# Layer 1 of a two-layer convolution kernel: a ring buffer for the spline features, a new layout for the SiLU scratch, shared row loads and another order of the DMA queue

## The chip, the core and the metric

The kernel runs on one core of one Trainium2 chip. The metric is the time of one execution on the device in microseconds (us); shorter is better. An execution is one program: it reads its inputs from HBM, computes both layers for all four images and writes the output back to HBM. A few tensors in HBM are scratch that one part of the program writes and a later part reads.

## The reference

The input x has 4 images of 16 channels of 256 by 256 in float32. There are two layers, each of which adds to x what it computes from a group-normalised x:

```python
# layer 0
x = x + _L0_conv_ref(_gn(x), conv_w, conv_b)   # 3x3 conv to 400 logits, softmax over 25 taps, weighted 5x5 sum
# layer 1
x = x + _L1_conv_ref(_gn(x), base_weight, spline_weight, spline_scaler, bias_weight)
...
    patches = _extract_patches(x, KSIZE, STRIDE, PAD)            # 3x3, zero padding
    bspl = _b_splines(patches, grid)                             # 8 cubic B-spline bases
    out = jnp.einsum('bjhwn,ijn->bihw', jax.nn.silu(patches), base_w)
    out = out + jnp.einsum('bjhwns,ijns->bihw', bspl, spl_w)
    out = out + bias_weight[None, :, None, None]
```

Layer 1, which the change is about, is thus a 3x3 convolution over 9 maps for each input channel: the SiLU of the normalised pixel and its 8 spline bases.

## The kernel before, in words

Layer 0 works in 64 strips (image, half of the rows, 32 columns). TensorE makes the logits (L773, L777), ScalarE their exponentials (L796), GpSimd multiplies them by the pixels (L801), VectorE sums (L677). The SyncE queue (SP) loads its operands ahead. The result of layer 0, x1, goes to an HBM scratch `x1s` (channel, row, column). In the last strips, `scales(0)` turns the statistics of image 0 into the scale and shift that layer 1 needs, one small step at a time.

Layer 1 works in 64 units: image b, and a block u of 16 rows. For unit n the code of `layer1` does, on several engines:

- `load_x(n)` (L867): one DMA of 2048 KB, x1s into `xt`. Each of the 16 channels is written to 8 partitions (128 in all), one for each spline basis, so each partition gets the same run of 16 rows, 16 KB. Three buffers, `xta`, `xtb`, `xtc`.
- `features(n)` (L902): on ScalarE the absolute value with scale and shift (L908), on both halves of the rows, then `spline` (L155): three activations on ScalarE (L158 to L160) and four operations on VectorE (L161 to L164). The result goes into a feature tile `fa`, `fb` or `fc` of 18 rows by 258 columns, the columns 0 and 257 holding padding.
- `halo(n)` (L911): the first two rows of a feature tile are the last two of the one before; a DMA from SBUF to SBUF copies them (L917), and GpSimd writes padding at the edge of an image.
- SiLU: `load_rows(n, xsp, "xs")` loads the unit's 16 rows in another layout (8 rows by 16 channels on the partitions, two DMAs of 128 KB), `silu` (L883) applies the activation in place on ScalarE three units ahead, `put_silu` (L887) writes it to the HBM scratch `sls` in two DMAs, and `load_silu(n)` (L894) reads it back in four DMAs, one for each of the four input rows of a pair of output rows, into `sl` (64 partitions). The scratch has 1 KB rows; the zero row above and below an image is written once, in layer 0 (L816).
- `outputs(n)` (L931): 96 matmuls on the features (L937) and 24 on `sl` (L945), in float32, into one PSUM tile.
- The residual: `load_rows(n, xrp, "xr")` loads the same 16 rows once more, `put` (L923), two units later, adds the PSUM tile, the bias and the residual on VectorE (L925) and stores the result in two DMAs (L927).

The order of all engines' queues is written by hand: `in_order` keeps the instructions of each engine in the order of the code. For SP a unit of the loop (L978 to L999) is: `load_x(n+2)`, halo of n, `put_silu(n+2)` (two DMAs), `xs` rows of n+5 (two), `xr` rows of n (two), the store of n-2 (two), `load_silu(n+1)` (four): 14 DMAs. In the built program there are eight semaphores for SP's DMAs, used in turn, and each DMA waits for the one before it on its own semaphore, so at most eight DMAs of this queue are under way. VectorE's order is: one step of `scales` for one of the images 1 to 3 (L980), features of n, then the `put` of n-2.

Of the kernel before, what the change touches and what calls it, by code (L numbers as in the profile page):

```python
# [33 lines left out]
def conv_preact_kernel(  # L34
# [14 lines left out]
    G = 8  # L49
# [27 lines left out]
    XA = 5  # L77
    NU = H // RU
    LAG1 = 2
# [12 lines left out]
    sls = [dram.tile([C, CP], F32, name=f"sls{b}") for b in range(B)]  # L92
# [33 lines left out]
    zrow = const.tile([C, W], F32, name="zrow")  # L126
    nc.gpsimd.memset(zrow, 0.0)
# [38 lines left out]
    def scales(b, psum):  # L166


        def small(n, name):
            return stat1.tile([P, n], F32, name=f"{name}_{b}", tag=name)  # L170

        mv = stat1.tile([P, G, 2], F32, name=f"mv_{b}", tag="mv")
        for g in range(G):
            nc.vector.bn_aggr(mv[:, g, :], st1[b][:, g].rearrange("p n s -> p (n s)"))
        yield
        ps = psum()[:, 0:G]
        nc.tensor.matmul(ps, lhsT=ones, rhs=mv[:, :, 0], start=True, stop=True)
        yield
        mean, d, rstd = small(G, "mean"), small(G, "d"), small(G, "rstd")
        q = stat1.tile([P, 6], F32, name=f"q_{b}", tag=f"q{b}")  # L180
        nc.vector.tensor_sub(d, mv[:, :, 0], ps)
        nc.vector.tensor_mul(mean, gsel_sb, ps)
        nc.vector.reduce_sum(q[:, 1:2], mean, AX.X)
        yield
        nc.scalar.activation(d, d, AF.Square)
        yield
        ps = psum()[:, 0:G]
        nc.tensor.matmul(ps, lhsT=ones, rhs=d, start=True, stop=False)
        nc.tensor.matmul(ps, lhsT=ones, rhs=mv[:, :, 1], start=False, stop=True)
        yield  # L190
        nc.vector.tensor_scalar(rstd, ps, EPS, None, ALU.add)  # L191
        yield
        nc.gpsimd.tensor_tensor(rstd, rstd, mhalf, ALU.pow)  # L193
        nc.gpsimd.tensor_mul(rstd, rstd, gsel_sb)
        yield
        nc.vector.reduce_sum(q[:, 0:1], rstd, AX.X)
        nc.vector.tensor_scalar(q[:, 1:2], q[:, 1:2], q[:, 0:1], -1.0, ALU.mult, ALU.mult)
        for k in range(2):
            nc.vector.tensor_scalar(q[:, 2 + k : 3 + k], q[:, k : k + 1], 2.5, None, ALU.mult)
        yield  # L200
        ps = psum()[:, 0:2]
        nc.tensor.matmul(
            ps, lhsT=sel.rearrange("p c s -> p (c s)"), rhs=q[0:C, 2:4], start=True, stop=True
        )
        yield
        nc.vector.tensor_copy(q[:, 4:5], ps[:, 0:1])
        nc.vector.tensor_add(q[:, 5:6], ps[:, 1:2], ub)
        sc[b] = tuple(q[:, k : k + 1] for k in (0, 1, 4, 5))
        yield
# [179 lines left out]
    with tc.tile_pool(name="prep0", bufs=2) as prep, tc.tile_pool(  # L389
# [91 lines left out]
        def prepare1():  # L481

            nc.gpsimd.tensor_mul(sw, sw, ss)
            wc = pre.tile([P, 3, nm], F32, name="wc")
            for d in range(3):
                nc.vector.tensor_reduce(
                    wc[:, d], sw[:, d].rearrange("p k j -> p j k"), AX.X, ALU.add
                )
            nc.vector.tensor_scalar(wc, wc, -1.0 / 6.0, None, ALU.mult)
            wb1 = pre.tile([nm, nm], F32, name="wb1")  # L490
            nc.vector.tensor_reduce(wb1, bw.rearrange("p k j -> p j k"), AX.X, ALU.add)
            for r in range(RT):
                nc.vector.tensor_copy(
                    wt[:, r : r + 3, :, r, :], wc.rearrange("p d (e o) -> p d e o", e=3)
                )
                nc.sync.dma_start(
                    ws[r * C : (r + 3) * C, :, r, :], wb1.rearrange("p (e o) -> p e o", e=3)
                )
# [96 lines left out]
    def layer0(shift):  # L595
# [4 lines left out]
        with tc.tile_pool(name=f"prep{arm}", bufs=2) as prep, tc.tile_pool(  # L600
# [136 lines left out]
            for n, (b, hf, s) in enumerate(strips):  # L737
                if (hf, s) == (0, 0):
# [3 lines left out]
                    if b == B - 1:  # L742
                        first_scales = scales(0, lambda: ptr.tile(
                            [P, QG, P], F32, name=f"ps0{arm}", tag="tp"
                        )[:, 0])
# [9 lines left out]
                for j in range(0, SW, JG):  # L755
# [55 lines left out]
                    if b == B - 1 and j == 0 and s > 0:  # L811
                        next(first_scales, None)
                if n == 0:
                    for t in sls:
                        for r in (0, H + 1):
                            nc.sync.dma_start(t[:, r * W : (r + 1) * W], zrow)  # L816
# [11 lines left out]
    def layer1(arm, last, marks):  # L828
# [3 lines left out]
        with ExitStack() as pools:  # L832
# [13 lines left out]
            XT, FT = [P, RU + 1, W], [P, RU + 2, W + 2]  # L846
            xt0, tmp0, xsp = fixed("xta", XT), temps("ta"), pool("xs", XA)
            f0, xrp = fixed("fa", FT), pool("xr", LAG1 + 2)
            tmp1, xt1, f1 = temps("tb"), fixed("xtb", XT), fixed("fb", FT)
            sl = fixed("sl", [RD * C, RU // RT, W + 2], 2)  # L850
            xtt, fb = xt0 + xt1 + fixed("xtc", XT), f0 + f1 + fixed("fc", FT)
# [12 lines left out]

            def load_x(n):  # L867
                b, u = units[n]
                lo, hi = span(u)
                nc.sync.dma_start(  # L870
                    xtt[n % 3][:, 0 : hi - lo, :],
                    rows(x1s[b], [[CP, C], [0, NS], [1, (hi - lo) * W]], u * RU - 1 + lo),
                )


            def load_rows(n, p, name):
                b, u = units[n]
                t = p.tile([P, 2, W], F32, name=f"{name}_{n}{arm}", tag=name)
# [4 lines left out]
            def silu(n, t):  # L883
                b, u = units[n]
                nc.scalar.activation(t, t, AF.Silu, scale=sc[b][0], bias=sc[b][1])

            def put_silu(n, t):  # L887
                b, u = units[n]
                for g in range(2):
                    nc.sync.dma_start(  # L890
                        rows(sls[b], [[W, 8], [CP, C], [1, W]], 1 + u * RU + 8 * g), t[:, g]
                    )

            def load_silu(n):  # L894
                b, u = units[n]
                for d in range(RD):
                    nc.sync.dma_start(
                        sl[n % 2][d * C : (d + 1) * C, :, 1 : W + 1],
                        rows(sls[b], [[CP, C], [RT * W, RU // RT], [1, W]], u * RU + d),
                    )  # L900

            def features(n):  # L902
                b, u = units[n]
                lo, hi = span(u)
                mid = (lo + hi + 1) // 2
                for (a, z), tmp in (((lo, mid), tmp0), ((mid, hi), tmp1)):
                    xt = xtt[n % 3][:, a - lo : z - lo]
                    nc.scalar.activation(xt, xt, AF.Abs, scale=sc[b][2], bias=sc[b][3])  # L908
                    spline(fb[n % 3][:, a:z, 1 : W + 1], xt, *(t[:, 0 : z - a, :] for t in tmp))

            def halo(n):  # L911
                b, u = units[n]
                f = fb[n % 3]
                if u == 0:
                    nc.gpsimd.tensor_copy(f[:, 0, :], pad)
                else:
                    nc.sync.dma_start(f[:, 0:2, :], fb[(n - 1) % 3][:, RU : RU + 2, :])  # L917
                if u == NU - 1:
                    nc.gpsimd.tensor_copy(f[:, RU + 1, :], pad)  # L919
# [3 lines left out]
            def put():  # L923
                b, u, yp, xr = waiting.pop(0)
                nc.vector.scalar_tensor_tensor(xr, yp, bias_sb, xr, ALU.add, ALU.add)  # L925
                for g in range(2):
                    nc.sync.dma_start(  # L927
                        rows(out[b], [[W, 8], [H * W, C], [1, W]], u * RU + 8 * g), xr[:, g]
                    )

            def outputs(n, xr):  # L931
                b, u = units[n]
                yp = py.tile([P, 2, W], F32, name=f"yp_{n}{arm}", tag="yp")
                M = RT * C
                for k, (d, e) in enumerate((d, e) for d in range(RD) for e in range(3)):
                    for t in range(NT):
# [3 lines left out]
                            rhs=fb[n % 3][:, t * RT + d : t * RT + d + 9 : 8, e : e + W],  # L940
                            start=k == 0, stop=False,
                        )
                for e in range(3):
                    for t in range(NT):
# [3 lines left out]
                            rhs=sl[n % 2][:, t : t + NT + 1 : NT, e : e + W],  # L948
# [6 lines left out]
                for b in range(1, B)  # L955
            ))
            load_x(0)
            ss = [load_rows(n, xsp, "xs") for n in range(XA)]
            load_x(1)
            nc.gpsimd.tensor_copy(pad, edge[:, 4:5].to_broadcast([P, W + 2]))  # L960
            for t in fb:
                for e in (0, W + 1):
                    nc.gpsimd.tensor_copy(
                        t[:, :, e : e + 1],
                        edge[:, 4:5].unsqueeze(2).to_broadcast([P, RU + 2, 1]),
                    )
            for t in sl:
                for e in (0, W + 1):
                    nc.gpsimd.memset(t[:, :, e : e + 1], 0.0)
            features(0)  # L970
            first_silu = len(nc.cur_bb.bb.instructions)
            for n in range(SA):
                t = ss.pop(0)
                silu(n, t)
                put_silu(n, t)
            load_silu(0)
            made = []
            for n in range(len(units)):  # L978
                if n > 0:
                    next(more, None)  # L980
                    features(n)
                if n + 2 < len(units):
                    load_x(n + 2)
# [3 lines left out]
                made = []  # L987
                if n + SA < len(units):
                    t = ss.pop(0)
                    silu(n + SA, t)  # L990
                    made.append((n + SA, t))
                if n + XA < len(units):
                    ss.append(load_rows(n + XA, xsp, "xs"))
                xr = load_rows(n, xrp, "xr")
                if len(waiting) >= LAG1:
                    put()
                if n + 1 < len(units):
                    load_silu(n + 1)
                outputs(n, xr)  # L999
            while waiting:  # L1000
                put()
# [57 lines left out]
```

## Time and profile before

| | |
|---|---|
| median of 3 runs | 3414.09 us (3395.18 to 3421.41) |
| the profiled execution's own time | 3413.86 us |
| its span, first to last instruction | 3412.1 us |
| busy, whole span: TensorE / VectorE / ScalarE / GpSimd | 2853.5 / 3100.7 / 2135.2 / 1935.3 us |
| granted TensorE clock, mean | 0.91 |
| DMA | 687.47 MB in 405554 packets, mean 201 GB/s |
| VectorE's last instruction of layer 0 / first of layer 1's features | 2102.50 us (L697; its statistics follow at 2104.82) / 2107.45 us (L161) |
| first `put` on VectorE / the 61st | 2157.55 us / 3367.25 us |

The span falls into three parts: up to about 130 us the inputs, statistics and weights, then layer 0 up to about 2107 us, then layer 1. "Busy" counts compute instructions; a DMA-issuing instruction on SP isn't counted as busy. The DMA share is the mean over the core's 16 DMA engines. A wait names the instruction or the DMA whose end came last before it ended. The DMA records of the trace hold each packet's start, duration and size.

### The profile page before, as it was taken

The numbers are of one execution on the slowest core, as the hardware profiler recorded it, in microseconds if no ns is written. First come the engines' busy times: TensorE is split into PE (matmuls) and PEld (weight loads), VectorE is DVE, ScalarE is ACT, GpSimd is POOL, SyncE is SP. The second block draws the span as 40 slices with busy tenths as digits, with TensorE's granted clock in tenths as the row PEclk, the third lists the DMA queues.
The fourth block names the chain that finished last, engine by engine and source line by source line (L and its number), as shares of the span: only waits on it lengthen the run. The fifth ranks groups of instructions, "written<-read, shape, count | busy, mean of one in ns | idle before, by whom it ended". The sixth has DMA issues, their size and how long they took to land.

```text
span 3412.1 us, 39823 instructions
## 1 busy us (share of the span) xinstructions
PE 2853.5 (84%) x14264; PEld 1509.4 (44%) x14264; DVE 3100.7 (91%) x1799; ACT 2135.2 (63%) x2233; POOL 1935.3 (57%) x647
## 2 busy tenths in 40 slices
PE   4499999999999999999999995677777777777778
PEld 3366665666655566566566552122222222222222
DVE  6599999999999999999999999877887888878886
ACT  6365654555644565554444446787887777778775
POOL 2299999999999999999999995000000000000000
PEclk7699999999999999999999997888888888888889
DMA  7998887888787798777766667888888888888885
GB/s 229 286 235 221 228 223 200 210 208 245 213 222 192 198 241 239 202 203 192 183 166 180 180 157 159 188 197 195 198 197 193 191 190 194 196 194 192 192 198 131
DMA packets 405554, 687.47 MB, mean 201 GB/s; under 512 B 47986, under 2 KB 274788, under 8 KB 397156
## 3 DMA queue, kind: packets, MB, share of 16 engines
q1 hardware_dynamic: 372324, 668.05, 78.6%
q10 hardware_dynamic: 33024, 16.78, 1.7%
q8 instruction: 117, 1.92, 0.3%
q14 instruction: 89, 0.73, 0.1%
HBM read 547.64 MB, written 121.15 MB: 196 GB/s over the span
## 4 chain that ended last, share of the span: by engine, by line
DVE 53%; DMA 34%; PE 5%; SPq 4%; issue 3%; ACT 1%; POOL 1%; ACTq 0%; DVEq 0%; POOLq 0%
DVE nd L677 45%; DMA xr<-x1s 8%; DMA sl<-sls 7%; DMA xs<-x1s 5%; DMA xtb<-x1s 4%; DMA xtc<-x1s 3%; PE lg L773 2%; DMA sls<-xs 2%; PE yp L937 1%; DMA xin<-in_x_dram 1%; DVE r L696 1%; DMA fc<-fb 1%; DVE st L711 1%; DVE nd L695 1%; SPq L880 1%
## 5 line engine op out<-in xcount | busy, mean ns | idle before, releaser
L773 PE MATMUL lg<-wm,am 128*128 128x400 f32 x4096 | 1748.4, 508 | 123.4 <-ACT e L796 109.2
L801 POOL TENSOR_TENSOR e<-e,u 128x1600 f32<-128x1600 f32 x512 | 1789.0, 3538 | 67.2 <-ACT e L796 66.8
L677 DVE TENSOR_REDUCE nd<-e 128x128 f32<-128x3200 f32 x512 | 1747.0, 3476 | 21.7 <-POOL e L801 21.6
L796 ACT ACTIVATE e<-lg 128x800 f32<-128x800 f32 x1024 | 815.6, 836 | 896.4 <-DVE nd L677 782.9
L777 PE MATMUL lg<-wn,an 97*128 97x400 f32 x2048 | 1358.5, 663 | 0.0
L773 PEld LDWEIGHTS lg<-wm,am 128*128 128x128 f32 x4096 | 766.3, 194 | 450.3 <-ACT e L796 159.6
L777 PEld LDWEIGHTS lg<-wn,an 97*128 97x128 f32 x2048 | 390.9, 191 | 309.8 <-issue 13.4
L937 PE MATMUL yp<-fa,wt 128*32 128x512 f32 x2112 | 278.8, 687 | 134.5 <-DMA fa<-fc 89.2
L937 PE MATMUL yp<-fb,wt 128*32 128x512 f32 x2016 | 259.7, 677 | 110.4 <-DMA fb<-fa 98.8
L937 PE MATMUL yp<-fc,wt 128*32 128x512 f32 x2016 | 260.7, 679 | 102.1 <-DMA fc<-fb 102.1
L919 POOL COPY fa<-pad 128x258 f32<-128x258 f32 x2 | 3.4, 1704 | 477.3 <-DMA xr<-x1s 315.5
L937 PEld LDWEIGHTS yp<-fa,wt 128*32 128x32 f32 x2112 | 82.6, 123 | 327.7 <-issue 279.7
L937 PEld LDWEIGHTS yp<-fb,wt 128*32 128x32 f32 x2016 | 79.4, 122 | 288.2 <-issue 288.2
L937 PEld LDWEIGHTS yp<-fc,wt 128*32 128x32 f32 x2016 | 79.6, 122 | 280.6 <-issue 274.0
L193 POOL TENSOR_TENSOR rstd<-rstd,mhalf 128x8 f32<-128x8 f32 x4 | 9.3, 2332 | 340.4 <-DVE rstd L191 340.4
L919 POOL COPY fc<-pad 128x258 f32<-128x258 f32 x1 | 1.5, 1474 | 319.6 <-DMA fa<-fc 319.6
L945 PE MATMUL yp<-sl,ws 64*32 64x512 f32 x1536 | 178.1, 592 | 0.0
L163 DVE TENSOR_TENSOR ta<-ta,ta 128x2048 f32<-128x2048 f32 (+1 forms) x64 | 147.3, 2302 | 0.0
L163 DVE TENSOR_TENSOR tb<-tb,tb 128x2048 f32<-128x2048 f32 x64 | 145.3, 2271 | 0.0
L908 ACT ACTIVATE xta<-xta,q 128x2048 f32<-128x2048 f32 (+2 forms) x44 | 92.0, 2090 | 82.0 <-DMA xta<-x1s 82.0
L908 ACT ACTIVATE xtb<-xtb,q 128x2048 f32<-128x2048 f32 (+2 forms) x42 | 87.8, 2091 | 83.7 <-DMA xtb<-x1s 83.7
L908 ACT ACTIVATE xtc<-xtc,q 128x2048 f32<-128x2048 f32 (+2 forms) x42 | 87.8, 2091 | 81.3 <-DMA xtc<-x1s 81.3
(184 smaller groups left out, 2605.0 us busy)
## 6 DMA issues: line engine op xcount, KB each, us to landing
am<-hst SPq DMA_DIRECT2D x512, 194.6 KB
u<-hs SPq DMA_DIRECT2D x320, 288.0 KB
an<-hsl SPq DMA_DIRECT2D x512, 129.8 KB
xtb<-x1s SPq DMA_DIRECT2D x19, 2048.0 KB
xtc<-x1s SPq DMA_DIRECT2D x19, 2048.0 KB
xta<-x1s SPq DMA_DIRECT2D x18, 2048.0 KB
am<-hst SPq DMA_DIRECT2D x256, 129.8 KB
sl<-sls SPq DMA_DIRECT2D x256, 128.0 KB
```

What stands on the lines that cost most here:

```text
L163: nc.vector.tensor_mul(s1, s1, r1)
L677: nc.vector.tensor_reduce(nd[:, :, j : j + JG, :], e.rearrange("p t j m c d -> p t j c m d"), AX.XY, ALU.add,)
L695: nc.vector.tensor_mul(nd[:, 0], nd[:, 0], r)
L696: nc.vector.scalar_tensor_tensor(r, nd[:, 0], 2.0, r, ALU.subtract, ALU.mult)
L711: nc.vector.bn_stats(st1[b][:, g, k, :], xc[:, g * GC : (g + 1) * GC, :].rearrange("p c w -> p (c w)"),)
L773: nc.tensor.matmul(lg[:, i, :NL], lhsT=am[:, o : o + P], rhs=wm.rearrange("p m c d -> p (m c d)"), start=True, stop=False,)
L777: nc.tensor.matmul(lg[:, i, :NL], lhsT=an[:, o : o + P], rhs=wn.rearrange("p m c d -> p (m c d)"), start=False, stop=True,)
L796: nc.scalar.activation(ev, lg[:, :, :NL], AF.Exp)
L801: nc.gpsimd.tensor_tensor(e[:, 1].rearrange("p j m c d -> p j (m c) d"), e[:, 0].rearrange("p j m c d -> p j (m c) d"), uv, ALU.mult,)
L908: nc.scalar.activation(xt, xt, AF.Abs, scale=sc[b][2], bias=sc[b][3])
L937: nc.tensor.matmul(yp[t * M : (t + 1) * M], lhsT=wt[:, d, e].rearrange("p r o -> p (r o)"), rhs=fb[n % 3][:, t * RT + d : t * RT + d + 9 : ...
L945: nc.tensor.matmul(yp[t * M : (t + 1) * M], lhsT=ws[:, e].rearrange("p r o -> p (r o)"), rhs=sl[n % 2][:, t : t + NT + 1 : NT, e : e + W], ...
```

## The change

All of it but two pieces lies in layer 1.

- The features of three units lie in one tile `ring` of 50 rows instead of three tiles of 18. A unit takes the 16 rows that its place (`place(n)`, 0, 16 or 32) points at, plus two; the two rows shared with the next unit are then the same memory, and the copying DMA remains only where the ring wraps, for about each third unit.
- The rows for SiLU and residual are loaded once, into `xr` (8 buffers); `silu` writes to a tile `ss` of its own (2 buffers), and `xr` is kept until the residual is added. Rows are now loaded four units ahead, not five and none.
- The scratch `sls` is split by even and odd rows, two planes for each channel, with a row pitch of 257 elements whose first element is zero; the eight rows that one partition of `sl` needs are then one run of 2057 elements (8228 bytes), zeros between rows included. `load_silu` is two DMAs of 32 partitions each, and the weights `ws` are put in the order of the rows that this gives. `put_silu` writes the rows to their planes.
- The zeros of the scratch are written in layer 0: in each of its first 40 strips one DMA of 32 by 13 rows of 257 elements from a tile of zeros, instead of eight small DMAs.
- `load_x` is two DMAs of half the rows.
- SP's order in a unit is: halo, `put_silu(n+2)` (two), `load_silu(n)` (two; before, that of n+1), first half of x for n+2, rows of n+4 (two), second half of x for n+2, store of n-2 (two).
- The addition of `put` on VectorE stands between the two halves of `features(n)`; the stores follow at the end of the unit.
- `scales` of image 1 runs in the last strips of layer 0 beside that of image 0, the other two in layer 1 with one step in every second unit, with tiles of their own for even and odd images.

The core of the diff:

```diff
-    XA = 5
+    XA = 4
+    SILU_ROWS = (3, 0, 1, 2)
+    ZP = 10
...
-    sls = [dram.tile([C, CP], F32, name=f"sls{b}") for b in range(B)]
+    HR, WS = H // 2 + 2, W + 1
+    sls = [dram.tile([2 * C, HR, WS], F32, name=f"sls{b}") for b in range(B)]
...
-                if n == 0:
-                    for t in sls:
-                        for r in (0, H + 1):
-                            nc.sync.dma_start(t[:, r * W : (r + 1) * W], zrow)
+                if n < B * ZP:
+                    t, r0 = sls[n // ZP], n % ZP * (HR // ZP)
+                    nc.sync.dma_start(
+                        t[:, r0 : r0 + HR // ZP],
+                        zero[0 : 2 * C, 0:WS].unsqueeze(1).to_broadcast([2 * C, HR // ZP, WS]),
+                    )
...
-            def load_x(n):
+            def load_x(n, half):
                 b, u = units[n]
-                lo, hi = span(u)
+                lo, hs = halves(u)
+                a, z = hs[half]
                 nc.sync.dma_start(
-                    xtt[n % 3][:, 0 : hi - lo, :],
-                    rows(x1s[b], [[CP, C], [0, NS], [1, (hi - lo) * W]], u * RU - 1 + lo),
+                    xtt[n % 3][:, a - lo : z - lo, :],
+                    rows(x1s[b], [[CP, C], [0, NS], [1, (z - a) * W]], u * RU - 1 + a),
                 )
...
             def put_silu(n, t):
                 b, u = units[n]
                 for g in range(2):
                     nc.sync.dma_start(
-                        rows(sls[b], [[W, 8], [CP, C], [1, W]], 1 + u * RU + 8 * g), t[:, g]
+                        bass.AP(
+                            tensor=sls[b].tensor,
+                            offset=sls[b].offset + (1 + u * RU // 2 + 4 * g) * WS + 1,
+                            ap=[[WS, 4], [HR * WS, 2 * C], [1, W]],
+                        ),
+                        t[:, g],
                     )

             def load_silu(n):
                 b, u = units[n]
-                for d in range(RD):
+                r0 = u * RU // 2
+                for p, r, dr in ((0, r0 + 2, C * HR - 2), (2 * C, r0 + 1, C * HR)):
                     nc.sync.dma_start(
-                        sl[n % 2][d * C : (d + 1) * C, :, 1 : W + 1],
-                        rows(sls[b], [[CP, C], [RT * W, RU // RT], [1, W]], u * RU + d),
+                        sl[n % 2][p : p + 2 * C],
+                        bass.AP(
+                            tensor=sls[b].tensor, offset=sls[b].offset + r * WS,
+                            ap=[[dr * WS, 2], [HR * WS, C], [1, RU // RT * WS + 1]],
+                        ),
                     )
...
             for n in range(len(units)):
+                if n % 2:
+                    next(more, None)
                 if n > 0:
-                    next(more, None)
-                    features(n)
-                if n + 2 < len(units):
-                    load_x(n + 2)
+                    features(n, put)
                 halo(n)
                 for m, t in made:
                     put_silu(m, t)
                 made = []
+                load_silu(n)
+                if n + 2 < len(units):
+                    load_x(n + 2, 0)
                 if n + SA < len(units):
-                    t = ss.pop(0)
-                    silu(n + SA, t)
-                    made.append((n + SA, t))
+                    made.append((n + SA, silu(n + SA, xr[n + SA])))
                 if n + XA < len(units):
-                    ss.append(load_rows(n + XA, xsp, "xs"))
-                xr = load_rows(n, xrp, "xr")
-                if len(waiting) >= LAG1:
-                    put()
-                if n + 1 < len(units):
-                    load_silu(n + 1)
-                outputs(n, xr)
+                    xr.append(load_rows(n + XA))
+                if n + 2 < len(units):
+                    load_x(n + 2, 1)
+                store()
+                outputs(n, xr[n])
```

## The prediction

> **What bounds the kernel now.** I read the page first, then a table of windows, SP's waits, SP's timeline and the trace's DMA packet records. The windows split the span:
>
> ```profile
> core 0: us, PE busy (x) PEld busy (x) DVE busy (x) ACT busy (x) POOL busy (x), PEclk, DMA share, GB/s
> 1200.00:1600.00 400.00, 377.64 (x1323) 244.00 (x1321) 399.11 (x184) 219.29 (x339) 385.69 (x119) 0.98 0.81 221
> ...
> 2160.00:3363.00 1203.00, 909.97 (x7176) 268.86 (x7168) 994.77 (x584) 943.15 (x537) 18.46 (x12) 0.84 0.88 195
> ```
>
> In layer 0 (first row) VectorE is busy 399 of 400 us. In layer 1 (second row) no engine is: VectorE 83%, ScalarE 78%, TensorE 76%, but the DMA engines are busy 88% on the mean. From the first addition of `put` (2157.55) to the 61st (3367.25) a unit takes 1209.7/60 = 20.16 us. VectorE needs 994.77 x 20.16/1203 = 16.67 us of it; where inputs had piled up, its additions stand 16.6 us apart (2184.41, 2201.05, 2217.69). So 3.5 us a unit are lost to transfers.
>
> SP's timeline and waits show how:
>
> ```profile
> 2620.31 0.59 SPq L870 DMA_DIRECT2D xta<-x1s  x1
> 2621.83 0.52 SPq L917 DMA_DIRECT2D fb<-fa  x1
> 2622.45 1.54 SPq L890 DMA_DIRECT2D sls<-xs  x2
> 2624.49 1.44 SPq L880 DMA_DIRECT2D xs<-x1s  x2
> 2626.41 6.36 SPq L880 DMA_DIRECT2D xr<-x1s  x2
> 2635.37 1.31 SPq L927 DMA_DIRECT2D out_dram<-xr  x2
> 2636.78 2.71 SPq L897 DMA_DIRECT2D sl<-sls  x4
> ```
> ```profile
> SPq L870 <- DMA xr<-x1s: 80.8, 55, 2.0
> SPq L927 <- DMA xtb<-x1s: 55.9, 19, 4.1
> SPq L917 <- DMA xr<-x1s: 55.6, 56, 1.3
> ...
> SPq L897 <- DMA xs<-x1s: 41.7, 79, 1.2
> SPq L880 <- DMA sl<-sls: 36.7, 101, 1.1
> ```
>
> Each wait is for the DMA eight places earlier in SP's order (the store L927 for the x load, the x load L870 for the first `xr`). Eight are under way, SP is held by their landing, not by a compute engine, and DMA engines always have work queued.
>
> The packet records give prices (2200 to 3300 us). An x packet of 16384 bytes takes 1269 ns on average with all 16 engines on x (208 GB/s together), but 642 to 749 ns when at most two are in flight beside row packets, 608 at least. Row packets of 1024 bytes run about 8.6 at a time, 192 GB/s, that is 43 ns on each of 8 engines. Halo packets of 2064 bytes take 149.
>
> [...] x, halo and `sl` have 16 outermost, the eight row DMAs 8, so 6x16 + 8x8 = 160 semaphore packets a unit; the records have 158 four-byte packets (all on 16 would give 224), and 8.6 row packets are in flight, not 16. So engines 0 to 7 carry more than 8 to 15. [...] 1 KB packets into 16 partitions take 106 to 141 ns and reach 106 to 173 GB/s.
>
> Check, engines 0 to 7, one unit: x 8 x 1.27 = 10.2; halo 8 x 0.15 = 1.2; rows (`xs`, `sls`, `xr`, `out`) 128 x 0.043 = 5.5; `sl` 2.8 (from 2638.9 to 2641.7). Sum 19.7 against 20.16: these eight engines bound layer 1.
>
> **The change, part by part,** on the DMA engines that will carry most. [...] Engine 0 (and 1), one unit:
> - One row load gone: 32 packets remain, 32 x 0.043 = 1.4. Store, unchanged: 1.4.
> - `put_silu`: 256 packets on 4 engines, 64 x 0.043 = 2.7 (before: 1.4). The rows now start at odd addresses (pitch 1028 bytes); no row shows such a write. Ends: 0 and +2.7 (double); I take 0.
> - First `sl` DMA: 16 packets of 8228 bytes. Half of 608 ns each if alone, 0.305, so 4.9; half of 1269 ns beside full x traffic, so 10.1. Second: 2 packets, 0.6 to 1.2.
> - x: 16 packets of 8 KB, 4.9 alone, 10.1 beside the others.
> - Halo: one unit in three, 8 x 0.15/3 = 0.4. Semaphores: 9 x 0.015 = 0.1.
>
> Alone: 1.4 + 1.4 + 2.7 + 4.9 + 0.6 + 4.9 + 0.4 + 0.1 = 16.4. The 34 large packets (10.4 us) stretch up to double while other engines move x. Those need 14/16 x 2.1 MB / 208 GB/s = 8.8 us in a unit. With unit time T, 10.4 us of work runs at half rate during a share 8.8/T: T = 6.0 + 10.4/(1 - 4.4/T), which T = 19.4 solves (6.0 + 13.4). Engines 2 and 3 stay at 1.4+1.4+2.7+1.2+10.1+0.5 = 17.3, engines 8 to 15 at 11.8. So engines 0 and 1 are the bound, and the unit falls from 20.16 to 19.4.
>
> The other edits cost or save nothing by themselves:
> - VectorE's waits for the steps of `scales` (L181, L191, L206: 100 us in nine waits) lose their reason with a step in every second unit. They were hidden: the x loads follow each other at 20 us through them. Without DMA cover they would have cost 100 us; the slack in other units repaid them.
> - `put` between the halves: the same 0.75 us, and it waits for a PSUM tile two units old; behind it stand the second half's four operations, and behind those the matmuls. The store lets SP go on half a unit earlier, and the next `put_silu`, `sl` and x issues queue behind it; ten DMAs a unit against eight under way leave each 15 us to land.
> - `load_silu(n)` no longer asks for `put_silu` of one iteration ago (L897's place behind 13 us of `sls` in the chain), and its user, the last 24 matmuls of the unit, comes 15 us later.
> - Zeros in layer 0: 40 DMAs of 26 packets on each engine, 26 x 0.046 = 1.2 us (double at most), on SP's queue ahead of the next `am` loads. SP waits 668.5 us there for TensorE to free `am` buffers, so it has room[...].
> - `scales` of image 1 in layer 0: one L174 group of 1.1 us and a dozen operations of 0.16, about 3 us on the busy VectorE; it leaves layer 1 where it was hidden. +3.
>
> Sum: 60 x (19.4 - 20.16) + 3 = -43, on the profiled execution's 3413.9 (span 3412.1, 1.8 around it): 3371. The median, 3414.1, stands at the same place. A unit of 0.1 us is worth 6 us; I say 3370.
>
> **Rivals.**
> 1. *VectorE becomes the bound.* If SP's order makes engines 0 and 1 do their large packets while the others are on rows or idle[...], the DMA side takes 16.4 us or less and VectorE's 16.67 decides: 60 x -3.49 + 3 = -206, 3207. For it: two lone x packets took 642 to 749 ns, and engines 2 to 15 have a third of their time free. Against it: eight DMAs in flight tie their x bursts to what engine 0 has just finished, so the meetings aren't random.
> 2. *Slower: the two engines meet the others' x always.* Place: engines 0 and 1, first `sl` DMA and x. If x stays at 1269 ns per 16 KB, T = 16.4 + 5.2 = 21.6, +86 and +3: 3503. It decides when the large packets lose over 3.8 us of a possible 10.4; my forecast has 3.0. The unaligned `put_silu` adds up to 2.7 to this side. For it: 16 large packets at once run at half rate all through the kernel's x phases.
> 3. *The change does little:* the unit stays near 20.2 because the removed row load and halos (2.6 us) are given back by `put_silu` and `sl`. That is the upper edge of my forecast, 3414.
>
> **Chances.** Forecast (T from 18.6 to 20.2, 3320 to 3415): 0.40. Rival 1 and what lies between (3205 to 3320): 0.29. Rival 2 (over 3415): 0.31. A measurement of this kernel tells about 1% (34 us) from no change; that bound, T = 19.6, cuts the forecast: 0.22 of it faster, 0.18 same; of rival 2 0.03 is same. So faster 0.51, same 0.21, slower 0.28. The range leaves out the outer part of both rivals: 3205 to 3500; the forecast's own is 3320 to 3415.
>
> **What would show it.** Right: units near 19.4 us, still longer than VectorE's 16.7; four-byte packets a unit of 8 put + 2 + 16 + 32 x + 32 rows and store = 90, plus 16 per halo; 8 KB packets near 305 ns when few are in flight and 630 when many; SP waiting for `sl`, x or `xr` landings; a mean DMA share well under 0.88 while SP still waits, since two engines are full and fourteen not. Wrong: VectorE over 95% in layer 1 (rival 1); `sl` packets beyond 600 ns and units over 20.2 (rival 2); idle time on VectorE in layer 0, where I put none.

## The result and the profile after

The changed kernel takes 3586.22 us (median of 4 runs, 3581.03 to 3590.83); the kernel before took 3417.75 us beside it. The ratio is 1.0499, 95% interval 1.0438 to 1.056: about 5% slower, where the forecast was 3370 and the range ended at 3500. From the first `put` (2154.11) to the 61st (3539.45) a unit takes 23.09 us, against 20.16 before and 19.4 forecast.

The windows of the changed kernel, in the same two stretches as before:

```profile
core 0: us, PE busy (x) PEld busy (x) DVE busy (x) ACT busy (x) POOL busy (x), PEclk, DMA share, GB/s
1200.00:1600.00 400.00, 376.18 (x1326) 243.46 (x1325) 399.11 (x183) 218.97 (x340) 386.19 (x119) 0.99 0.83 228
2160.00:3363.00 1203.00, 879.03 (x6260) 245.31 (x6256) 867.34 (x498) 823.05 (x470) 9.32 (x10) 0.79 0.66 152
```

Layer 0 is as it was. In layer 1 every compute engine is less busy than before, and so is the mean DMA engine: 0.66 against 0.88. A mean share that falls while all else idles suggests that few DMA engines carry the load. SP's timeline shows where the queue stands (start, duration of the issues, line):

```profile
2794.03 7.12 SPq L965 DMA_DIRECT2D out_dram<-xr  x2
2805.61 2.74 SPq L910 DMA_DIRECT2D sls<-ss  x2
2808.64 2.28 SPq L923 DMA_DIRECT2D sl<-sls  x2
2811.02 0.91 SPq L888 DMA_DIRECT2D xtc<-x1s  x1
2812.36 1.22 SPq L898 DMA_DIRECT2D xr<-x1s  x2
2813.62 0.54 SPq L888 DMA_DIRECT2D xtc<-x1s  x1
2815.12 5.10 SPq L965 DMA_DIRECT2D out_dram<-xr  x2
2827.57 3.95 SPq L910 DMA_DIRECT2D sls<-ss  x2
```

After the stores SP stands still (4.5 us before 2805.61, 7.4 us before 2827.57), then `put_silu` and all loads go out within 9 us. SP's waits from 2160 to 3500 us (line, what was waited for: us, times, longest) name what held it:

```profile
SPq L910 <- DMA sl<-sls: 252.5, 51, 10.8
SPq L950 <- DMA sl<-sls: 104.0, 18, 7.7
SPq L965 <- DMA sls<-ss: 99.5, 116, 1.5
```

Count eight places back from the first `put_silu` (store, store, x, row, row, x, `sl`, `sl`): in a unit without a halo copy it is the first `sl` load of the unit before, the one that the prediction put on engines 0 and 1. In a unit with one, the halo copy (L950) stands there. The other engines' waits in the same stretch tell the same from their side:

```profile
ACT ss L904 <- DMA xr<-x1s: 422.2, 58, 8.9
...
PE yp L983 <- DMA sl<-sls: 259.0, 53, 9.1
```

And the chain of waits, first before, then after (only the line that splits it by source line):

```profile
DVE nd L677 45%; DMA xr<-x1s 8%; DMA sl<-sls 7%; DMA xs<-x1s 5%; DMA xtb<-x1s 4%; DMA xtc<-x1s 3%; PE lg L773 2%; DMA sls<-xs 2%; PE yp L937 1%; DMA xin<-in_x_dram 1%; DVE r L696 1%; DMA fc<-fb 1%; DVE st L711 1%; DVE nd L695 1%; SPq L880 1%
```
```profile
DVE nd L682 38%; DMA sl<-sls 16%; PE lg L777 6%; DMA xtb<-x1s 4%; DMA xta<-x1s 3%; DMA xtc<-x1s 3%; DMA xr<-x1s 2%; SPq L910 2%; PE yp L983 2%; DMA out_dram<-xr 2%; DMA sls<-ss 2%; PE lg L781 2%; SPq L923 1%; DVE st L716 1%; DVE r L701 1%
```

The `sl` load's share rises from 7% to 16%. The trace's packet records (they don't name the engine) fit this: between 2250 and 3450 us fewer than two packets are in flight in 0.1% of the time, exactly two in 9.4%, and the mean of sixteen engines is 66% busy. That is what two engines that always have work would leave.

How many engines work on a DMA is read from the same records (2200 to 3150 us). In the changed kernel exactly 2, 4, 8 and 16 packets are in flight in 9.4, 12.4, 8.5 and 23.9% of the time, but 3 and 5 only in 5.4 and 4.6%; before, 2 and 4 are in flight in 0.1 and 0.2%, and rows alone stand most often at eight (22.6% of the time without any larger packet). Four-byte packets a unit are as many as the slowest dimensions of the DMAs add up to: 158.6 for 160 before, 94.8 for 95.3 after, where the first `sl` load counts 2, each `put_silu` 4, and the second `sl` load, of 32, 16. "Engines 0 and 1", "0 to 3" and "0 to 7", here and in the prediction, are only names for sets of two, four and eight. That the smaller set lies in the larger is assumed; the records fit it: beside exactly two `sl` packets the rows, where there are any, stand most often at six (27% of that time; eight in 6%), and the x packets, where there is no row, at fourteen (69%).

### The profile page after: what moved, and what is told of

It reads as the page before. It is cut to its first block, busy times and chain, and to the rows that moved or that the text cites. A ratio compares the mean times of both kernels' runs of the same rounds, so it can differ in the third digit from the quotient of the medians.

```text
span 3588.6 us, 39515 instructions
## 1 busy us (share of the span) xinstructions
PE 2955.8 (82%) x14264; PEld 1519.1 (42%) x14264; DVE 3102.4 (86%) x1799; ACT 2132.1 (59%) x2233; POOL 1923.3 (54%) x638
## 3 DMA queue, kind: packets, MB, share of 16 engines
q10 hardware_dynamic: 33024, 16.78, 1.5%
## 4 chain that ended last, share of the span: by engine, by line
DVE 44%; DMA 36%; PE 11%; SPq 4%; issue 3%; ACT 2%; POOL 1%; ACTq 0%; DVEq 0%; POOLq 0%
DVE nd L682 38%; DMA sl<-sls 16%; PE lg L777 6%; DMA xtb<-x1s 4%; DMA xta<-x1s 3%; DMA xtc<-x1s 3%; DMA xr<-x1s 2%; SPq L910 2%; PE yp L983 2%; DMA out_dram<-xr 2%; DMA sls<-ss 2%; PE lg L781 2%; SPq L923 1%; DVE st L716 1%; DVE r L701 1%
## 5 line engine op out<-in xcount | busy, mean ns | idle before, releaser
L975 PE MATMUL yp<-ring,wt 128*32 128x512 f32 x6144 | 788.7, 664 | 139.4 <-DMA ring<-ring 88.5
L975 PEld LDWEIGHTS yp<-ring,wt 128*32 128x32 f32 x6144 | 231.2, 120 | 723.6 <-issue 688.4
L983 PE MATMUL yp<-sl,ws 64*32 64x512 f32 x1536 | 287.1, 899 | 280.8 <-DMA sl<-sls 265.1
L904 ACT ACTIVATE ss<-xr,q 128x512 f32<-128x512 f32 x64 | 52.0, 814 | 439.4 <-DMA xr<-x1s 431.2
L983 PEld LDWEIGHTS yp<-sl,ws 64*32 64x32 f32 x1536 | 62.8, 140 | 465.4 <-DMA sl<-sls 292.9
L163 DVE TENSOR_SCALAR xta<-xta 128x2048 f32<-128x2048 f32 (+2 forms) x44 | 53.7, 1221 | 131.6 <-ACT ta L161 131.6
L163 DVE TENSOR_SCALAR xtb<-xtb 128x2048 f32<-128x2048 f32 (+2 forms) x42 | 51.3, 1222 | 128.1 <-ACT ta L161 128.1
L166 DVE TENSOR_TENSOR ring<-ta,ta 128x2048 f32<-128x2048 f32 (+1 forms) x64 | 147.8, 2310 | 2.5
L166 DVE TENSOR_TENSOR ring<-tb,tb 128x2048 f32<-128x2048 f32 x64 | 145.6, 2275 | 2.6
L162 ACT ACTIVATE ta<-ta 128x2048 f32<-128x2048 f32 (+1 forms) x64 | 122.4, 1913 | 0.0
```

The source lines that it names most:

```text
L162: nc.scalar.activation(s1, r1, AF.Square, scale=2.0)
L163: nc.vector.tensor_scalar(t, t, 2.0, 2.0, ALU.min, ALU.subtract)
L166: nc.vector.tensor_add(f, s2, s1)
L975: nc.tensor.matmul(yp[t * M : (t + 1) * M], lhsT=wt[:, d, e].rearrange("p r o -> p (r o)"), rhs=ring[:, r0 + t * RT + d : r0 + t * RT + d ...
L983: nc.tensor.matmul(yp[t * M : (t + 1) * M], lhsT=ws[:, e].rearrange("p r o -> p (r o)"), rhs=bass.AP(tensor=sl[n % 2].tensor, offset=sl[n ...
```

## The experiments

Times are medians beside runs of the kernel before on the same chip; "unit" is (61st `put` - first `put`)/60. Theory 1: engines 0 and 1 are full because the first `sl` load runs on them alone, and its packets meet the x packets of the other engines. Its rivals: a wait in SP's order, the x packets themselves, the other edits.

| run | us | ratio to before, 95% interval | unit |
|---|---|---|---|
| e1: after, `sl` load split to 16 engines | 3309.34 | 0.9693 (0.9644 to 0.9743) | 18.57 |
| e2: after, `put_silu` moved behind the x loads | 3643.48 | 1.0671 (1.0618 to 1.0725) | 23.90 |
| e3: after, scratch of before | 3392.24 | 0.9926 (0.9907 to 0.9944) | 19.92 |
| e4: after, x copies from distinct addresses | 3593.61 (one run) | - | 23.12 |
| e5: after, x dealt in 128 rows | 3360.64 | 0.9847 (0.9801 to 0.9894) | 19.34 |
| e6: before, one row load | 3339.61 | 0.9761 (0.9698 to 0.9823) | 19.07 |
| e7: before, new scratch | 3701.58 | 1.0847 (1.0809 to 1.0886) | 24.72 |
| e8: e1 with whole x | 3244.08 | 0.9507 (0.9473 to 0.9541) | 17.30 |
| e9: after with whole x | 3550.39 | 1.0391 (1.0363 to 1.0419) | 22.29 |
| e10: e7, `sl` load split to 16 engines | 3512.40 | 1.0278 (1.025 to 1.0305) | 21.80 |
| e11: e8, `put_silu` on 16 engines | 3231.31 | 0.9463 (0.9436 to 0.949) | 17.17 |
| e12: after, nearly no x | 3205.24 | 0.9381 (0.9349 to 0.9414) | 16.72 |
| e13: e1, halves of x side by side | 3210.94 | 0.9405 (0.9372 to 0.9438) | 16.78 |
| e14: e1, `put_silu` on 16 engines | 3298.57 | 0.9661 (0.9628 to 0.9695) | 18.35 |
| e15: e10, `put_silu` on 16 engines | 3384.83 | 0.9913 (0.9879 to 0.9948) | 19.66 |

### The load on two engines: e1, e7, e12, e2

**e1** splits the first `sl` load in two DMAs whose slowest dimension is 16:

```diff
-for p, r, dr in ((0, r0 + 2, C * HR - 2), (2 * C, r0 + 1, C * HR)):
+for p, r, m in ((0, r0 + 2, C), (C, C * HR + r0, C), (2 * C, r0 + 1, 2 * C)):
     nc.sync.dma_start(
-        sl[n % 2][p : p + 2 * C],
+        sl[n % 2][p : p + m],
...
-            ap=[[dr * WS, 2], [HR * WS, C], [1, RU // RT * WS + 1]],
+            ap=[[HR * WS, m], [1, RU // RT * WS + 1]],
```

> Edit: the first SiLU load is split into its two rows, two DMAs of 16 partitions with 16 outermost each, same bytes, one DMA more a unit. Theory 1 (two DMA engines carry the first SiLU load and set the unit's time): its 16 large packets leave engines 0 and 1, which keep about 20 us a unit or less (rows 1.4, store 1.4, put 2.9, SiLU 3.6, x 8 to 10, rest 0.5), so the time falls by 180 us or more, to 3400 or below. Theory 2 (SP is held because put_silu waits for a SiLU load eight DMAs earlier, whatever engines carry it): the wait stays, moved by one place, and one DMA more a unit of a queue of eight makes it longer: no gain, 3550 to 3650.

Measured: 3309.34, 277 us less than the changed kernel, with one DMA more in a unit and not a byte moved elsewhere. The groups of TensorE's instructions from 2160 to 3500 us (line, op, names, shapes, count; busy, mean ns; idle before them, and what ended it), after and then e1:

```profile
L983 PE MATMUL yp<-sl,ws 64*32 64x512 f32 x1384 | 265.9, 922 | 268.6 <-DMA sl<-sls 259.0 <-DMA sls<-ss 9.6
```
```profile
L983 PE MATMUL yp<-sl,ws 64*32 64x512 f32 x1488 | 172.4, 592 | 0.0
```

The wait of the SiLU matmuls for `sl` is gone, and the kernel is faster than the one before. So what the change loses goes with the way in which this one load is dealt to the engines.

**e7** is the converse: the kernel before with the new scratch, its `load_silu` and `put_silu`, and no other edit.

> Edit: the kernel before with the new SiLU scratch alone (planes, puts on 4 outermost, two loads, the first with 2 outermost, zeros in layer 0). Theory 1: engines 0 and 1 carry x 10, halo 1.2, two row loads and the store 4.1, puts 2.8, SiLU 8 to 11: 26 to 29 us a unit, 3750 to 3950. Theory 2 (the new order of the queue does the harm, not the load): with the old order about as before, 3350 to 3480.

Measured: 3701.58, 288 us more than before, and a unit of 24.72 us, where theory 1 had 26 to 29 us and 3750 to 3950: the right way, but too much. The scratch alone does more harm than the whole change; the other edits win some of it back.

**e12** takes the other party of the meeting away:

```diff
 b, u = units[n]
+if n > 2 and u > 0:
+    return
```

> The changed kernel with x loaded only for the first three units and the first unit of each image (the features of the other units are made of what the tiles hold, so they are not the reference's); everything else, the sl load on two engines too, is kept. Theory 1 (sl packets of 8228 bytes are slow because other engines move x at the same time): they fall to about 310 ns each, engine 0 needs 6.0 + 18 x 0.31 = 11.6 us a unit, VectorE's 16.7 decides, about 3210. Rival (they are slow by themselves, sixteen neighbouring partitions of SBUF on two engines): they stay near 560 ns. Time about the same in both; the packets tell.

Measured: 3205.24, unit 16.72, VectorE's own time. From the packet records, all `sl` packets of 8228 bytes that had at most one other `sl` packet beside them, that is those of the two-engine load:

```
kernel   packets a unit   mean ns   median ns
after         33.4          631        621
e5            34.0          453        440
e12           33.2          345        313
```

Two engines with 16 each have 32 of them in a unit; one or two of the second load's are caught with them. Without x they take 313 ns at the median, with it 621. So they aren't slow by themselves: the other engines' x doubles them. Between 2200 and 3150 us 81% of them have eight or more x packets beside them in the changed kernel (628 ns on average), while 86% have none in e12 (326 ns). VectorE is the bound in e12 (windows, columns as above):

```profile
2200.00:3150.00 950.00, 847.19 (x6842) 228.79 (x6834) 941.45 (x537) 901.48 (x515) 18.12 (x11) 0.95 0.31 91
```

**e2** tests the rival that SP's order is at fault. `put_silu`, which SP was seen waiting at, moves behind the second half of x, ahead of the store; the two-engine load stays.

> Edit: put_silu moved from ahead of the SiLU load to behind the second half of x, ahead of the store; the loads are those of the change. Theory 1 (two engines full): engines 0 and 1 carry the same packets in another order, so the unit stays at 22 to 24 us, 3540 to 3640. Theory 2 (the wait of put_silu on the SiLU load holds SP): put_silu now waits for a store, so at least half of the 250 us of that wait goes, 3460 or below.

Measured: 3643.48, slower still, and 3 us above the range of theory 1. The wait of `put_silu` for `sl` is gone from SP's table, but another has come (2200 to 3150 us):

```profile
SPq L923 <- DMA sls<-ss: 152.7, 38, 4.6
```

The `sl` load now waits for `put_silu`, so the time of e2 alone doesn't clear SP's order. The packet records say more: two or more packets are still in flight in 99.2% of the time, and 96% of the two-engine load's packets (81% in the changed kernel) now have eight or more x packets beside them and take 680 ns. With e1 this speaks for the wait at L910 as the place where the full engines showed, not their cause.

### Why x takes twice its time: e4 and e5

Both keep x's bytes and change the addresses that it is read from, which no longer move with the unit; the features are then not the reference's. **e4** gives each of the 8 copies of a channel its own address, with the channels still slowest; **e5** makes 128 the slowest dimension of the source.

```diff
-rows(x1s[b], [[CP, C], [0, NS], [1, (z - a) * W]], u * RU - 1 + a),
+bass.AP(..., ap=[[CP, C], [8256, NS], [1, (z - a) * W]]),      # e4
+bass.AP(..., ap=[[CP // NS, P], [1, (z - a) * W]]),            # e5
```

> Edit: each of the 128 partitions of x reads addresses of its own in its channel (step 8256 elements where it was 0), so the features are not those of the reference; outermost size 16, packet sizes and everything else as changed. If large packets run at half rate because eight partitions read the same addresses, x packets fall to 310 to 350 ns with all engines on x, SiLU packets too, and the unit to 17 to 18.5 us (3250 to 3330). If it is the way the engines meet on the SBUF side, nothing changes: x packets near 590 ns, about 3590.

> Edit: as e4, but the 128 partitions of x read one evenly stepped pattern, so that the outermost size is 128 on both sides and not 16 (the features are not those of the reference). If the way x is dealt to the engines makes them meet on the SBUF side, x packets of 8 KB fall from about 590 ns toward 310 to 400, SiLU packets too, engines 0 and 1 need 17 to 19 us a unit and the time falls to 3210 to 3340. If large packets run at half rate whatever the pattern: no change, about 3590.

Measured: e4 3593.61, as the changed kernel. e5 3360.64, 226 us less, but 21 us above the range that was expected. In e5 an 8 KB x packet takes 336 ns at the median, where it took 605; while 14 or more x packets are in flight, all packets under way move 337 GB/s, against 228 in the changed kernel (2200 to 3150 us). The two-engine `sl` packets fall to 453 ns on average. So reading the same address eight times isn't what halves x; how x is dealt out is. The records name neither engine nor partition, so which pieces of e5 run side by side, and whether the SBUF side has a part in it, is not shown.

### What else the scratch does: e3, e10, e15

**e3** is the changed kernel with the scratch, `put_silu` and `load_silu` (four DMAs) of before, kept in the changed order.

> Edit: the SiLU scratch is that of before (one plane of 1 KB rows, puts on 8 outermost, four loads of 16 partitions in 1 KB packets); ring, single row load, halves of x and order stay as changed. Theory 1: engines 0 to 7 carry x 8 to 10, rows 1.4, store 1.4, put 1.4, SiLU 2.8, halo 0.4, about 17.5 us a unit: 3230 to 3300. Theory 2 (order and the queue of eight): 12.3 DMAs a unit against eight in flight, so SP waits stay; 3450 or above. Theory 3 (the ring or the halves hurt): above 3400 too, but with SP waiting for compute engines.

Measured: 3392.24, 194 us less than the changed kernel: in the changed order too the scratch is what harms. But it lies between the ranges of theories 1 and 2 and is only 25 us under the 3417.75 of before, although the single row load alone is worth 74 us (e6 below). Something else in the changed kernel costs time as well; e13 below shows one such thing, on e1. **e10** is e7 with the split load of e1, **e15** is e10 with `put_silu` dealt to 16 engines as well:

```diff
-for g in range(2):
-    ... ap=[[WS, 4], [HR * WS, 2 * C], [1, W]] ..., t[:, g]
+for i in range(4):
+    ... ap=[[HR * WS, 2 * C], [4 * WS, 2], [1, W]] ..., t[2 * C * i : 2 * C * (i + 1)]
```

> The kernel before with the new SiLU scratch alone, its first sl load split in two DMAs on 16 engines each; put_silu on four engines. Engines 0 to 3 per unit: x 8 x 1.27 = 10.2, halo 1.2, three row DMA pairs on eight engines 4.1, put_silu 2.7, sl 4 packets of 0.6 = 2.4, semaphores 0.2: 20.8, against 19.7 by the same sum before. Theory 1: the harm of the new scratch (287 us in the kernel with it alone) is nearly all the two-engine load, so 3400 to 3460 here. Rival (rows at odd addresses in HBM cost double): 3560 or more.

> The kernel before with the new SiLU scratch alone, sl load split on 16 engines, put_silu as four DMAs on 16 engines. Engines 0 to 7 per unit: x 10.2, halo 1.2, three row pairs 4.1, put_silu 16 x 0.043 = 0.7, sl 2.4, semaphores 0.2: 18.8, against 20.8 with put_silu on four. If the four engines make the remaining 96 us: 3320 to 3420. If rows at odd addresses make it: 3480 or more, since these stay.

Measured: e10 3512.40, e15 3384.83. Of the 288 us of the scratch alone, the split takes 189 back and the put on 16 engines another 128; then the kernel is 32 us better than before (3417.07 beside e15). The expectation of e10 was too low: its own sum (20.8 against 19.7, 1.1 us a unit) gives 66 us, not the 44 at most that it named; measured were 96. From e10 to e15 the sum says 2.0 us a unit, measured are 2.14 (21.80 - 19.66). That is 45 ns for each of the 48 row packets that an engine no longer has, the price of an ordinary row (43); at twice that price, as the rival has it for rows at odd addresses, it would have been 4.1.

### The halves of x and their place: e8, e9, e11, e13, e14; and e6

**e6** adds only the single row load to the kernel before.

> Edit: the kernel before with the single row load alone (rows four units ahead, SiLU into a tile of its own). Theory 1 (the fullest DMA engines set the unit): engines 0 to 7 lose 32 row packets of 43 ns, 1.4 us a unit, perhaps more because SP's queue of eight covers more of a unit of 12 DMAs: 3300 to 3340. Theory 2 (a unit is set by SP's order and landings): less than 1 us a unit, above 3360.

Measured: 3339.61, 74 us less; the prediction's 1.4 us a unit is 84 us.

**e8** is e1 with x in one DMA, at the place of the first half; **e9** the same on the changed kernel.

> Edit: e1 with x in one DMA a unit again (10.3 DMAs a unit, not 11.3). If halves help because half of x is asked for half a unit earlier: slower than e1 by 0.3 to 1 us a unit, 3330 to 3370. If eight DMAs in flight hold SP in e1, fewer DMAs make it faster: 3250 to 3300. If engines 0 to 3 simply carry 18.6 us of packets: the same within 15 us, 3295 to 3325.

> The changed kernel with each unit's x in one DMA again (16384-byte packets, issued where the first half stood); the sl load on two engines is kept. Theory 1 (engines 0 and 1 are full and meet the x of the others): their bytes are the same, so the unit stays near 23.1 us and the time within 25 us of 3586. Rival (the halves cost a place among the eight DMAs in flight, as the 65 us between the two kernels with the split sl load seem to say): about 3520.

Measured: 65 us less than e1 (e8, 6 us under the range of its second case), 36 us less than the changed kernel (e9). My theory 1 had e9 within 25 us of 3586 and missed: the halves do cost. Three runs on e1 and e8 narrow down why. **e13** keeps the halves and moves the second next to the first:

```diff
-    load_x(n + 2, 0)
+    for half in range(2):
+        load_x(n + 2, half)
...
-if n + 2 < len(units):
-    load_x(n + 2, 1)
```

**e11** is e8, and **e14** is e1, with `put_silu` as in e15.

> The kernel with the split sl load, with both halves of x issued next to each other at the place of the first half. If the place of the second half (behind two row loads) costs the 65 us: the time of whole x, 3244 within 20. If the extra DMA among the eight in flight costs it: 3309 stays, within 20.

> The kernel with the split sl load and whole x, with put_silu as four DMAs of 32 partitions on 16 engines in place of two of 128 partitions on 4 engines. If engines 0 to 3 still bind at 17.3 us a unit: the unit falls to VectorE's 16.7 and the time to about 3205. If the compute engines bind already: 3244 stays, within 15. If SP's issues and the eight DMAs in flight bind (two more DMAs a unit, each of 32 partitions): slower, 3290 or more.

> The kernel with the split sl load and halves of x at their two places, with put_silu as four DMAs of 32 partitions on 16 engines. If the halves cost time only because engines 0 to 3 are full with put_silu on four engines: 3231 within 20, as with whole x. If they cost it by themselves: 3290 or more.

Measured: e13 3210.94 (13 us under its range), e11 3231.31 (13 us under e8, within what its expectation called the same), e14 3298.57. So in e1 it is neither the extra DMA (e13 has it) nor the four engines of the put (e14 is rid of them, and its 11 us lie inside the intervals of the two). It is the place of the second half: 98 us between e1 and e13, whose instructions are otherwise the same. In place, the halves are even better than whole x (e13 against e8: 33 us). SP's waits from 2200 to 3150 us, e1 and then e13:

```profile
SPq L910 <- DMA xta<-x1s: 44.7, 10, 5.3
SPq L888 <- DMA sls<-ss: 44.0, 50, 1.5
SPq L965 <- DMA sls<-ss: 43.3, 51, 1.8
SPq L888 <- DMA xtc<-x1s: 39.9, 14, 4.1
SPq L888 <- DMA xtb<-x1s: 36.7, 13, 4.1
SPq L888 <- DMA xta<-x1s: 19.8, 7, 4.0
```
```profile
SPq L898 <- DMA sls<-ss: 63.1, 55, 1.6
SPq L965 <- DMA sls<-ss: 58.2, 57, 1.8
SPq L910 <- ACT xta L939: 43.6, 14, 4.0
SPq L910 <- ACT xtb L939: 40.0, 11, 4.2
```

In e1 the x loads (L888) wait 140 us. Eight places before the first half stands the last unit's second half, eight before the second half the first `put_silu` of its own unit. In e13 those places hold a row load and a store, and no wait of L888 is among the rows; `put_silu` (L910) now waits for ScalarE instead.

The packets changed too. From 2200 to 3150 us a unit's packets take 258 us of engine time in e1 and 237 in e13, though they are the same packets: 1 KB rows take 68 ns on average in e1 and 52 in e13, x packets of 8 KB 614 and 582. In e1 the row loads are issued between the halves; its rows with eight or more large packets (x or `sl`) beside them take 77 ns, those of e13 53. And in both kernels four or more packets are always in flight. So the place of the second half may cost through the price of the packets beside it as well as through SP's waits; these runs don't separate the two. The window of e13, columns as above:

```profile
2200.00:3150.00 950.00, 842.50 (x6820) 230.21 (x6812) 938.98 (x536) 896.40 (x512) 15.83 (x10) 0.96 0.88 210
```

VectorE is busy 939 of 950 us: rival 1's bound, with the DMA share of the kernel before and 8% more bytes a second (210 GB/s against 195). e13 is the fastest complete kernel, 5.9% under the kernel before and 6 us from the run with nearly no x.

## Why the prediction was wrong, point by point

**Right.** The bound of the kernel before, engines 0 to 7: eight or more packets were in flight in 98% of the time from 2200 to 3150 us, and e6 takes 1.4 us a unit of rows off them and gains 74 us (it also has two DMAs less in a unit). The number of engines that each DMA of the change runs on, an estimate from its slowest dimension (2 for the first `sl` load, 4 for `put_silu`): 94.8 four-byte packets a unit, against 90 and a third of 16; two packets in flight as the floor, in e1 four (e13 has the same floor with VectorE as its bound, so the floor alone proves none). That engines 0 and 1 would be the bound. The DMA share "well under 0.88". The 3 us for the earlier `scales`, with the zeros at nothing: in the profiled executions layer 1's first features start on VectorE at 2110.01 us, against 2107.45 before. (The first `put` comes earlier all the same, 2154.11 against 2157.55, because it now stands between the halves of `features`.) The rows at odd addresses at nothing (e10 against e15).

**The step that failed** is the stretch: "10.4 us of work runs at half rate during a share 8.8/T", the large packets meeting the others' x at random. They don't meet at random. Of the packets of the two-engine load 81% had eight or more x packets beside them. SP issues the `sl` load right ahead of the first half of x (2808.64 and 2811.02 above), so engines 0 and 1 do their 16 `sl` packets each while the fourteen others do x. The `sl` packets took 0.631 us each, all of the doubling, and most of the two engines' own x came when the others were through: 25 of their 32 x packets a unit had at most one other beside them and took 0.363 us (that these are theirs is assumed). With these the working of the prediction gives 6.0 + 16 x 0.631 + 2 x 0.48 for the second load + 12.5 x 0.363 + 3.5 x 0.6 = 23.7 us; measured were 23.09. The stretch was put at 3.0 us and was 6.7 (23.1 - 16.4). The sum keeps the rows at 43 ns, while the 1 KB packets of the changed kernel take 46 at the median and 65 on average, so that it comes within 0.6 us doesn't prove each term.

The profile before held the hint: rival 2's "always" needs only the order of SP's queue. I had it at 0.31, and sized it by one of the two groups of packets, x, at 5.2 us: 3503. It was the other group, `sl`, that doubled in full, and x was slowed in part. The mechanism was rival 2's, its size beyond it.

**A second step failed** beside it: "The other edits cost or save nothing by themselves". The halves and the new order were called cheap because "ten DMAs a unit against eight under way leave each 15 us to land". That looked at the count, and not at which DMA stands eight places earlier or at what the packets meet. With the load on two engines it was that load, for `put_silu`; with it split, the place of the second half still costs 98 us (e1 against e13).

**Rival 1** was there to be had: with the load split and the halves side by side, the unit is 16.78 us and the time 3210.94, where rival 1 said 3207. What stood between the change and it was the shape of one DMA and the place of another.

**Open.** Why an x packet takes 605 ns dealt in 16 and 336 dealt in 128; whether the place of the second half acts through SP's waits or through dearer packets beside it, since e1 against e13 shows the cost and not its path; what slows e2 beyond the changed kernel; and what makes the last 0.86 us between e15's unit and its sum.

## What to carry to other kernels

Before counting the bytes of a DMA, look at the slowest dimension of both its patterns: here a 2, 4, 8 or 16 there showed as so many packets in flight at once. Fewer, larger packets (2 DMAs for 4, 8 KB runs for 1 KB) lost 288 us here (e7): splitting the DMA that ran on two engines won 189 of them back, dealing the one on four to sixteen another 128. In the changed kernel the split alone won 277. Then sum the load of the fullest engine, with the price that its packets have beside what the queue issues next to them (for `sl` 621 ns, not 313), not an average of alone and crowded. And where a queue has a fixed number of DMAs under way (eight here), count back that many places from each load: moving one half of x two places changed what it waited for and what it ran beside, and the time by 98 us.

## What the runs showed of the hardware

- An x packet of 8 KB takes 605 ns at the median when the source's slowest dimension is the 16 channels, and 336 ns when it is 128; with 14 or more x packets in flight all packets together then move 228 and 337 GB/s. Reading one address eight times or eight different ones made no difference (3586.22 and 3593.61 us).
- A packet of 8228 bytes of the two-engine load takes 313 ns at the median with nearly no x about (e12), and 621 in the changed kernel, where other engines load x. The two-engine load loses as much to the others' x as x loses to itself (605 ns for 8192 bytes, 307 at least).
- The granted TensorE clock of layer 1 was lower in the kernels whose TensorE waits more: 0.79 in the changed kernel (TensorE busy 73%) and 0.84 before (76%), 0.95 in e12 and 0.96 in e13 (both 89%). No run here tests whether the clock adds to their time.
- Rows of 1 KB with eight or more large packets beside them took 77 ns on average in e1 and 53 in e13.
